# Second mixture of experts: six result buffers, rows six tiles at a time, sums in step with the tiles, and the last thirteen tiles behind a jump

## The chip, the cores and the metric

The kernel is one program on one core of a Trainium2 chip. The metric is the device time of one execution, in microseconds. Three executions of the kernel before took 852.63, 846.68 and 850.48 us; the median is 850.48 us. The profile is of a further execution.

## What is computed

The model has two layers; each adds an attention-like block and then a mixture of experts to x, of shape 16 x 128 x 256, float32. The change touches only the mixture of the second layer. There 2048 tokens (16 blocks of 128) choose 6 of 32 experts each. Cut to what matters:

```python
idx, w = _route(xf, Wr, br)                  # 2048 tokens, 6 of 32 experts, weights
gate = zeros((T, E)).at[arange(T)[:, None], idx].add(w)
def step(acc, ew):                           # over the 32 experts
    w1, w2, g = ew
    h = jnp.square(jax.nn.relu(xf @ w1.T)) @ w2.T
    return (acc + g[:, None] * h, None)
acc, _ = jax.lax.scan(step, zeros_like(xf), (W1, W2, gate.T))
x = x + jnp.tanh(g_ffn[1]) * (shared + acc)
```

xf is the normalised x. W1 is 128 x 256 for each expert and W2 256 x 128. Which experts a token takes depends on the data.

## The kernel before, in words

The kernel computes an expert only for the tokens that chose it. For each of the 16 blocks the router's result gives every (token, choice) a place in a table `sent` in device memory, sorted so that each tile of 128 rows belongs to one expert; GpSimd scatters the normalised rows there (line 961). A row carries the six expert numbers and the six places to which its results go. An expert's last tile may be partly filled, so up to NT1 = 16 x 6 + 31 = 127 tiles exist, and the program runs all 127, whatever the data; tiles without tokens write into a part of the result table that nobody reads. `state["used"]` holds the number of rows that were given out, tiles times 128.

The loop over tiles is written out in the program, `for t in range(NT1)`. Its steps and their lines in the profile:

- Every GRP = 4 tiles, SP loads the rows of four tiles (`got`, L1131, pool tag "big", 4 buffers) and ScalarE loads four weight offsets into registers (L1123). VectorE then finds the place of each row's result (`mine`, `to_f`, `to`, L1135 to L1145).
- Every two tiles (a pair): ScalarE copies each tile's expert weights out of the resident table (`wt`, L1155); TensorE turns the rows (L1158); VectorE copies them out of PSUM (`xts`, L1160); TensorE multiplies by W1 (`eh`, L1165); ScalarE takes the relu (`er`, L1173); VectorE multiplies relu by its input (`ehs`, L1175); TensorE multiplies by W2 (`eo`, L1177); ScalarE copies the result to SBUF (`ey`, L1185, three buffers).
- For each tile, GpSimd scatters 128 result rows of 1 KB to their places in the table `parts` (L1186). This is an indirect DMA, issued on GpSimd's queue.
- The sums. The blocks are in GROUPS of 4, 4, 4, 2, 1 and 1. All results of a group's blocks lie in the first last_tile(c) = 6 x (last block + 1) + 31 tiles. `combine(c)` stands six tiles behind that (or behind the last tile). For each block of the group SP loads three parts of 128 x 2 x 256 (`part`, L1109, four buffers), VectorE does six multiply-and-adds into x (L1115), and SP stores the block (L1118).

A framework puts these on the engines. Each engine works through its own queue in order. A scheduler sets that order when the program is built, close to the program's order with some interleaving; waits are semaphores that the framework adds, for data and for buffers to come free. [...]

Of the kernel before, what the change touches and what calls it, by code (L numbers as in the profile page):

```python
# [11 lines left out]
I32 = mybir.dt.int32  # L12
# [31 lines left out]
GRP = 4  # L44
# [7 lines left out]
def flamingo(ctx: ExitStack, tc: tile.TileContext, a: dict, out: bass.AP):  # L52
# [1039 lines left out]


    results, summed = [], []
    chunk = 0
# [5 lines left out]
    def combine(c):  # L1101

        n = P * TOPK1
        for b in range(*GROUPS[c]):
            for k0 in range(0, TOPK1, 2):
                part = work.tile([P, 2, D], F32, tag="act", name=f"part{b}_{k0}", bufs=4)
                at = NT1 * P + b * n
                src = parts[at : at + n, :].rearrange("(p k) d -> p k d", k=TOPK1)
                load = nc.sync.dma_start(out=part, in_=src[:, k0 : k0 + 2])  # L1109
                for ins in results[last_tile(c) :]:  # L1110
                    tc.declare_no_dep(load.ins, ins.ins, reason="later tiles have no row of a chunk that is summed")
                after(load, results[: last_tile(c)], "a chunk's results come from any of the first tiles")
                summed.append(load)
                for k in range(2):
                    V.scalar_tensor_tensor(  # L1115
                        xs[b], part[:, k, :], gates[:, b, k0 + k : k0 + k + 1], xs[b], ALU.mult, ALU.add
                    )
            nc.sync.dma_start(out=out[b], in_=xs[b])  # L1118

    for t in range(NT1):  # L1120
        if t % GRP == 0:
            n = min(GRP, NT1 - t)
            offsets = nc.values_load_multi_w_load_instructions(  # L1123
                table[0:1, t : t + n],
                engines=[mybir.EngineType.Activation],
                min_val=0,
                max_val=(E1 - 1) * W1_ROW,
                skip_runtime_bounds_check_because="the table holds numbers of experts times their weights' size",
            )[1]
            rows = work.tile([P, GRP, ROW], F32, tag="big", name=f"got{t}", bufs=BIGS)[:, :n]  # L1130
            load = nc.sync.dma_start(out=rows, in_=sent[t * P : (t + n) * P, :].rearrange("(g p) d -> p g d", p=P))  # L1131
            after(load, scatters, "a tile's rows come from any batch")

            mine = small.tile([P, GRP, TOPK1], F32, tag="mine", name=f"mine{t}", bufs=4)[:, :n]
            V.tensor_tensor(  # L1135
                mine,
                rows[:, :, D : D + TOPK1],
                owner[:, t : t + n].unsqueeze(2).to_broadcast([P, n, TOPK1]),
                ALU.is_equal,
            )  # L1140
            V.tensor_tensor(mine, mine, rows[:, :, D + TOPK1 :], ALU.mult)
            to_f = small.tile([P, GRP], F32, tag="to_f", name=f"to_f{t}", bufs=3)[:, :n]
            V.tensor_reduce(to_f, mine, AX.X, ALU.add)
            to = small.tile([P, GRP], U32, tag="to", name=f"to{t}", bufs=8)[:, :n]
            V.tensor_tensor(to, to_f, aside[:, t : t + n], ALU.max)  # L1145

        if t % 2 == 0:
            pair = range(t, min(t + 2, NT1))
            m = len(pair)
            tp = bank(("tr", "sc")[t // 2 % 2], f"xt{t}", 2)  # L1150
            eh = bank("mm", f"eh{t}", 2)
            eo = bank("so", f"eo{t}", 2)
            wt = work.tile([P, 2, W1_ROW], F32, tag="xT", name=f"wt{t}", bufs=4)
            for i, u in enumerate(pair):
                S.copy(wt[:, i], wts[:, bass.ds(offsets[u % GRP], W1_ROW)])  # L1155
                for kc in range(KC):
                    at = i * D + kc * P
                    T.transpose(tp[:, at : at + P], rows[:, u % GRP, kc * P : (kc + 1) * P], ident)  # L1158
            xt = work.tile([P, 2 * D], F32, tag="h", name=f"xts{t}", bufs=3)
            V.tensor_copy(xt[:, : m * D], tp[:, : m * D])  # L1160

            for i in range(m):
                for kc in range(KC):
                    cols = slice(kc * P, (kc + 1) * P)
                    T.matmul(  # L1165
                        eh[:, i * P : (i + 1) * P],
                        lhsT=wt[:, i, cols],
                        rhs=xt[:, i * D + kc * P : i * D + (kc + 1) * P],
                        start=(kc == 0),
                        stop=(kc == KC - 1),  # L1170
                    )
            r = work.tile([P, ROW], F32, tag="row", name=f"er{t}", bufs=8)[:, : m * P]
            S.activation(r, eh[:, : m * P], AF.Relu)  # L1173
            h = work.tile([P, D], F32, tag="xn", name=f"ehs{t}", bufs=3)[:, : m * P]
            V.tensor_tensor(h, r, eh[:, : m * P], ALU.mult)  # L1175
            for i in range(m):
                T.matmul(  # L1177
                    eo[:, i * D : (i + 1) * D],
# [74 lines left out]
```

## Time and profile before

| | |
|---|---|
| median of three runs | 850.48 us |
| profiled execution, time | 854.49 us |
| its span, first to last instruction | 852.7 us |
| mean granted TensorE clock | 0.918 |
| first row load of the second mixture issued | 644.65 us |
| first scatter starts | 657.22 us |
| 114th scatter starts | 820.48 us |
| 127th and last scatter starts | 841.60 us |
| last store issued | 850.03 us |
| scatters of results | 127, median 969 ns on GpSimd, 4.2 us from issue to landing |
| row loads | 31 of 536 KB and one of 402 KB |
| part loads | 48 of 256 KB, landing 2.7 / 2.8 us (min / median) |
| multiply-and-adds of the sums | 96 |

How to read it: times within the execution run from the start of the span. The time of an execution is a little longer than its span (854.49 against 852.7). A line of a group shows the source line, engine, operation, out<-in, shapes and count, then busy time and mean duration in ns of one, then the idle time before these instructions and who ended it.

### The profile page before, as it was taken

How to read it: one execution, taken by the hardware profiler on the slowest of the kernel's cores; microseconds unless marked ns; L12 is line 12 of the kernel's file. 1: busy time of each engine (PE TensorE's matmuls, PEld its weight loads, DVE VectorE, ACT ScalarE, POOL GpSimd, SP SyncE). 2: the span in 40 equal slices, each digit the busy share in tenths (PEclk: the TensorE clock that was granted, in tenths of full speed). 3: DMA queues.
4: the chain of work that ended last, by engine and by line, in shares of the span. 5: the costliest groups of instructions: out<-in, count | busy, mean ns of one | idle time of the engine just before them, and what ended most of it. 6: DMA issues, size and time to landing. Idle time of an engine off the chain costs nothing.

```text
span 852.7 us, 12578 instructions
## 1 busy us (share of the span) xinstructions
PE 747.0 (88%) x4032; PEld 524.1 (61%) x4032; DVE 548.6 (64%) x1660; ACT 375.4 (44%) x814; POOL 345.8 (41%) x339
## 2 busy tenths in 40 slices
PE   6999978989999999999899989698787989788862
PEld 3444444577675787565568657455456878677851
DVE  5999994337336755669647955756764546665675
ACT  2010046124424766552445344245435767666651
POOL 3766604200606000011640173046452767665663
PEclk8999979989999999999969969759978999998996
DMA  8999996122523233711331142523125657888586
GB/s 271 328 364 262 271 254 161 36 80 75 179 93 104 66 104 94 188 29 35 107 90 32 30 120 70 149 65 103 52 78 164 232 196 230 270 287 278 190 270 207
DMA packets 136513, 132.47 MB, mean 155 GB/s; under 512 B 43392, under 2 KB 119968, under 8 KB 136320
## 3 DMA queue, kind: packets, MB, share of 16 engines
q1 hardware_dynamic: 122576, 93.40, 39.3%
q0 software_dynamic: 13776, 38.23, 12.6%
q8 instruction: 32, 0.52, 0.3%
q14 instruction: 33, 0.27, 0.1%
q10 hardware_dynamic: 96, 0.05, 0.0%
HBM read 66.01 MB, written 65.62 MB: 154 GB/s over the span
## 4 chain that ended last, share of the span: by engine, by line
PE 49%; DVE 20%; DMA 11%; issue 7%; POOL 6%; ACT 5%; ACTq 0%; POOLq 0%; SPq 0%; DVEq 0%
PE y L328 7%; PE sc L844 5%; PE gu L771 4%; POOL parts L1186 4%; DMA part<-parts 4%; PE pg L606 3%; PE pu L606 3%; PE pt L865 3%; DMA parts<-ey,to 3%; PE os L658 3%; PE eo L781 3%; PE eo L1177 2%; DMA got<-sent 2%; PE avT L879 2%; ACT ex L858 2%
## 5 line engine op out<-in xcount | busy, mean ns | idle before, releaser
L1186 POOL DMA_INDIRECT parts<-ey,to x127 | 125.1, 985 | 74.4 <-ACT ey L1185 38.8
L961 POOL DMA_INDIRECT sent<-row,dst x96 | 93.3, 972 | 135.3 <-DVE dst L598 103.8
L858 ACT ACTIVATE ex<-sc,mn 128x128 f32<-128x128 f32 x256 | 71.8, 381 | 51.6 <-DVE mn L852 51.5
L801 POOL DMA_INDIRECT part<-parts,places x32 | 31.2, 975 | 143.7 <-DMA keys<-in_ctxT 86.2
L328 PE MATMUL y<-kv,toe 128*128 128x512 f32 x192 | 85.3, 599 | 0.0
L1177 PE MATMUL eo<-wt,ehs 128*128 128x256 f32 x254 | 68.9, 408 | 18.2 <-DVE ehs L1175 18.0
L320 POOL TENSOR_TENSOR kv<-cT 128x1024 f32<-128x1024 f32 x32 | 60.6, 1895 | 38.2 <-PE y L328 33.5
L1155 ACT COPY wt<-wts 128x512 f32 x127 | 72.2, 618 | 4.5 <-DVE x L622 1.5
L714 POOL DMA_INDIRECT sent<-row,places x32 | 31.2, 975 | 104.5 <-DVE places L493 41.0
L1165 PEld LDWEIGHTS eh<-xts,wt 128*128 128x128 f32 x508 | 69.4, 206 | 5.5 <-issue 2.5
L1165 PE MATMUL eh<-xts,wt 128*128 128x128 f32 x508 | 70.7, 291 | 1.2 <-DVE xts L1160 1.1
L606 PE MATMUL pg<-xT_s,wts 128*128 128x512 f32 (+1 forms) x160 | 66.4, 536 | 0.5 <-DVE silu L421 0.4
L606 PE MATMUL pu<-xT_s,wts 128*128 128x512 f32 (+1 forms) x160 | 64.0, 520 | 2.2 <-DVE row L200 2.2
L1177 PEld LDWEIGHTS eo<-wt,ehs 128*128 128x128 f32 x254 | 47.1, 200 | 28.3 <-DVE ehs L1175 18.4
L658 PE MATMUL os<-wts,hs 128*128 128x256 f32 x256 | 63.3, 382 | 0.0
L844 PE MATMUL sc<-keys,xT_at 32*128 32x256 f32 x256 | 61.6, 446 | 0.0
L328 PEld LDWEIGHTS y<-kv,toe 128*128 128x128 f32 x192 | 36.1, 193 | 41.5 <-issue 29.4
L1115 DVE SCALAR_TENSOR_TENSOR x<-part,gates,x 128x256 f32<-128x256 f32 x96 | 44.5, 479 | 23.4 <-DMA part<-parts 22.8
L1185 ACT COPY ey<-eo 128x512 f32<-128x512 f32 x64 | 37.2, 583 | 49.4 <-DMA parts<-ey,to 18.7
L1160 DVE COPY xts<-xt 128x512 f32<-128x512 f32 x64 | 43.1, 681 | 22.3 <-PE eh L1165 11.4
L658 PEld LDWEIGHTS os<-wts,hs 128*128 128x128 f32 x256 | 47.7, 191 | 15.2 <-issue 9.4
L852 DVE TENSOR_REDUCE mn<-sc 128x4 f32<-128x512 f32 x64 | 42.3, 682 | 16.8 <-PE sc L844 16.5
(246 smaller groups left out, 1393.6 us busy)
## 6 DMA issues: line engine op xcount, KB each, us to landing
sent<-keys SPq DMA_DIRECT2D x1, 17018.0 KB
got<-sent SPq DMA_DIRECT2D x31, 536.0 KB
part<-parts SPq DMA_DIRECT2D x48, 256.0 KB
sent<-keys SPq DMA_DIRECT2D x2, 2944.0 KB
got<-sent SPq DMA_DIRECT2D x22, 256.0 KB
parts<-ey SPq DMA_DIRECT2D x22, 256.0 KB
wts<-in_sw SPq DMA_DIRECT2D x3, 1024.0 KB
wts<-in_w SPq DMA_DIRECT2D x3, 1024.0 KB
```

The lines of the kernel that those rows point to most:

```text
L320: G.tensor_tensor(kv, c[:, :, hs].unsqueeze(3).to_broadcast(full), c[:, :, hs].unsqueeze(2).to_broadcast(full), ALU.mult)
L328: T.matmul(y[:, lb * TOK : (lb + 1) * TOK], lhsT=t[:, off : off + P], rhs=kv[:, kc * HALF : (kc + 1) * HALF].rearrange("p b i j -> p (b i ...
L606: T.matmul(ps, lhsT=w(kc), rhs=xT[:, kc, :n], start=(kc == 0), stop=(kc == KC - 1))
L658: T.matmul(o[:, k * D : (k + 1) * D], lhsT=hs[j][:, t * P : (t + 1) * P], rhs=wC[:, j, :], start=False, stop=(j == SH0 - 1 and k == len(ts ...
L844: T.matmul(scs[r][:, kc * D : (kc + 1) * D], lhsT=xT[rows, kc, cols], rhs=kz[rows, kc].rearrange("p m t -> p (m t)"), start=False, stop=(k ...
L858: S.activation(ex[:, i, :], scs[r][:, at : at + P], AF.Exp, bias=mn[:, i : i + 1], scale=-1.0)
L961: ins = G.indirect_dma_start(out=sent[:, :], out_offset=bass.IndirectOffsetOnAxis(ap=dst[:, t, k : k + 1], axis=0), in_=row, in_offset=None,)
L1115: V.scalar_tensor_tensor(xs[b], part[:, k, :], gates[:, b, k0 + k : k0 + k + 1], xs[b], ALU.mult, ALU.add)
L1155: S.copy(wt[:, i], wts[:, bass.ds(offsets[u % GRP], W1_ROW)])
L1165: T.matmul(eh[:, i * P : (i + 1) * P], lhsT=wt[:, i, cols], rhs=xt[:, i * D + kc * P : i * D + (kc + 1) * P], start=(kc == 0), stop=(kc == ...
L1177: T.matmul(eo[:, i * D : (i + 1) * D], lhsT=h[:, i * P : (i + 1) * P], rhs=wt[:, i, KC * P :], start=True, stop=True,)
L1186: ins = G.indirect_dma_start(out=parts[:, :], out_offset=bass.IndirectOffsetOnAxis(ap=to[:, t % GRP : t % GRP + 1], axis=0), in_=y[:, t % ...
```

## The change

1. GRP becomes 6: rows of six tiles in a load, six offsets at a time, owner steps on six tiles. The owner steps are put behind the pair's other work in the program, and the first of them must follow the copy `xts` of the group's first pair.
2. `ey` takes its buffers in turn from two tags of three buffers each: six pairs of tiles can hold results.
3. The sums of groups 0, 1 and 2 (blocks 0 to 11) are no longer fetched group-wise in `combine`. After a tile, one part is fetched (two for group 2) if the tile lies at least last_tile + 6 in; it waits for the results up to five tiles back, and is summed three tiles later (or when more than two wait).
4. The tile loop becomes a function `tiles1(t0, t1)`. Tiles 0 to 113 (SURE = 114) always run. Then all engines load `used` into a register, and tiles 114 to 126 run only if more than 114 x 128 rows were given out. On the other side of the jump the semaphores are raised by what the tiles left out would have raised; GpSimd first waits for the scatters before it raises theirs.
5. Blocks 12 to 15 are summed behind that jump by `sum_last`: three loads into one buffer ("big"), six scalings by the gates on ScalarE in place, one reduce over the six on VectorE, one add into x, one store.

The built program has in SP's queue, behind the jump: block 12's first load, the store of block 10, 12's other loads, 13's first, the store of block 11, 13's and 14's loads, the store of block 12, 15's loads, three stores. On VectorE seven of the old sums, of blocks 10 and 11, stand behind the jump as well.

The diff, cut to its core:

```diff
-GRP = 4
+GRP = 6
+SURE = 114
+FEW = 3
...
+    used_i = base.tile([P, 1], I32, tag="used_i", name="used_i")
+    V.tensor_copy(used_i, state["used"])
...
-    def combine(c):
-        n = P * TOPK1
-        for b in range(*GROUPS[c]):
-            for k0 in range(0, TOPK1, 2):
-                part = work.tile([P, 2, D], F32, tag="act", name=f"part{b}_{k0}", bufs=4)
...
-                for k in range(2):
-                    V.scalar_tensor_tensor(
-                        xs[b], part[:, k, :], gates[:, b, k0 + k : k0 + k + 1], xs[b], ALU.mult, ALU.add
-                    )
-            nc.sync.dma_start(out=out[b], in_=xs[b])
+    def load_results(part, b, k0, n_tiles):
...
+        load = nc.sync.dma_start(out=part, in_=src[:, k0 : k0 + 2])
...
+        after(load, results[:n_tiles], "a chunk's results come from any of the first tiles")
+        summed.append(load)
+    todo = [(b, k0) for b in range(GROUPS[FEW][0]) for k0 in range(0, TOPK1, 2)]
+    fetched = []
+    def fetch(t):
+        b, k0 = todo.pop(0)
+        part = work.tile([P, 2, D], F32, tag="act", name=f"part{b}_{k0}", bufs=4)
+        load_results(part, b, k0, min(t - 5, len(results)))
+        fetched.append((t, b, k0, part))
+    def add_fetched():
+        _, b, k0, part = fetched.pop(0)
+        for k in range(2):
+            V.scalar_tensor_tensor(xs[b], part[:, k, :], gates[:, b, k0 + k : k0 + k + 1], xs[b], ALU.mult, ALU.add)
+        if k0 + 2 == TOPK1:
+            nc.sync.dma_start(out=out[b], in_=xs[b])
+    def sum_last(b):
+        part = work.tile([P, TOPK1, D], F32, tag="big", name=f"part{b}", bufs=BIGS)
+        for k0 in range(0, TOPK1, 2):
+            load_results(part[:, k0 : k0 + 2], b, k0, len(results))
+        for k in range(TOPK1):
+            S.activation(part[:, k, :], part[:, k, :], AF.Copy, scale=gates[:, b, k : k + 1])
+        s = work.tile([P, D], F32, tag="xn", name=f"sum{b}", bufs=3)
+        V.tensor_reduce(s, part.rearrange("p k d -> p d k"), AX.X, ALU.add)
+        V.tensor_tensor(xs[b], xs[b], s, ALU.add)
+        nc.sync.dma_start(out=out[b], in_=xs[b])
-    for t in range(NT1):
+    def tiles1(t0, t1):
+        for t in range(t0, t1):
...
-            y = work.tile([P, 2, D], F32, tag="ey", name=f"ey{t}", bufs=3)
+                y = work.tile([P, 2, D], F32, tag=("ey", "got0")[t // 6 % 2], name=f"ey{t}", bufs=3)
...
+                follow(ins, turned_rows, "not needed before")
...
-        while chunk < len(GROUPS) and t + 1 >= min(NT1, last_tile(chunk) + 6):
-            combine(chunk)
-            chunk += 1
+            while fetched and (fetched[0][0] <= t - 3 or len(fetched) > 2):
+                add_fetched()
+            for _ in range(2 if todo and group(todo[0][0]) + 1 == FEW else 1):
+                if todo and t + 1 >= last_tile(group(todo[0][0])) + 6:
+                    fetch(t)
+    tiles1(0, SURE)
+    while fetched:
+        add_fetched()
+    used = nc.values_load(used_i[0:1, 0:1], min_val=0, max_val=NT1 * P, ...)
+    with tc.If(used > SURE * P):
+        tiles1(SURE, NT1)
+    for b in range(GROUPS[FEW][0], B):
+        sum_last(b)
```

## Prediction

> **What bounds the kernel now.** I read the page first (span 852.7 us), then the chain of waits. From 643 us on the chain stays in the second mixture, so I took that stage alone: the busy time in three stretches, GpSimd's timeline, the waits, the end of the chain, and the groups by shape.
>
> ```profile
> 657.20:736.30 79.10, 71.63 (x490) 64.73 (x488) 39.75 (x126) 57.38 (x119) 57.20 (x60) 0.98 0.67 210
> 736.30:841.60 105.30, 79.71 (x488) 70.39 (x488) 71.54 (x198) 62.53 (x126) 66.96 (x68) 0.92 0.82 267
> 841.60:852.70 11.10, 0.00 (x0) 0.00 (x0) 4.33 (x9) 0.00 (x0) 0.96 (x1) 0.50 0.39 134
> ```
>
> Columns: stretch, length, then busy us and instructions of PE, weight loads, DVE, ACT, POOL, the granted clock, DMA share, GB/s. The first stretch has tiles and no sums, the second both, the third only the last sums. No engine is full in the second, yet its tiles are slower.
>
> ```profile
> 657.22 0.96 POOL L1186 DMA_INDIRECT parts<-ey,to  x1 [14.17 <-ACT ey L1185]
> 658.49 0.97 POOL L1186 DMA_INDIRECT parts<-ey,to  x1 [0.31 <-issue]
> ...
> 740.57 1.19 POOL L1186 DMA_INDIRECT parts<-ey,to  x1 [3.34 <-ACT ey L1185]
> ...
> 841.60 0.97 POOL L1186 DMA_INDIRECT parts<-ey,to  x1 [0.30 <-issue]
> ```
>
> Each tile is one GpSimd scatter, 0.97 us and 0.30 us to the next: 1.275 us. From the first start (657.22) to the 127th (841.60) are 184.38 us; 126 x 1.275 is 160.65, so stalls are 23.7 us. To the 114th (820.48) the same sum gives 163.26 - 144.08 = 19.2 us of stalls, only about 3.8 of them before tile 60, where the sums begin.
>
> ```profile
> POOL parts L1186 <- ACT ey L1185: 38.8, 19, 14.2
> DVE mine L1135 <- DMA got<-sent: 30.7, 17, 4.8
> ...
> DVE x L1115 <- DMA part<-parts: 22.8, 14, 3.8
> ACT ey L1185 <- DMA parts<-ey,to: 18.7, 11, 4.0
> ```
>
> The stalls are waits for ey (the 14.2 is the start). ey comes late for two reasons: its three buffers are not yet scattered (18.7 us), and VectorE stands at a sum whose rows have not landed (22.8), with the next tiles' copies queued behind it; the 30.7 us at mine block ehs in the same way.
>
> ```profile
> 841.60 2.41 DMA parts<-ey,to
> ...
> 844.14 2.75 DMA part<-parts
> ...
> 846.91 0.49 DVE x L1115
> ...
> 849.51 0.48 DVE x L1115
> ```
>
> So the tail behind the last scatter's start is 11.1 us: landing, load, six sums, the store.
>
> ```profile
> L1115 DVE SCALAR_TENSOR_TENSOR x<-part,gates,x 128x256 f32<-128x256 f32 x96 | 44.5, 479 | 23.4 <-DMA part<-parts 22.8
> ...
> L406 DVE TENSOR_REDUCE mask_e<-eq_e 128x128 f32<-128x768 f32 x3 | 4.4, 1456 | 0.0
> ...
> L596 DVE TENSOR_REDUCE dstf<-eq_e 128x24 f32<-128x768 f32 x3 | 2.8, 945 | 0.0
> ```
>
> These three price the old and the new sum.
>
> **Part by part, on the profiled execution.**
>
> *Is the jump taken?* Counting the reference's routing on its inputs, tokens per expert rounded up to 128 give 113 tiles. SURE is 114, so the last 13 are left out: 13 x 1.275 = **-16.6 us** on the GpSimd queue, which paces the stage.
>
> *Rows six at a time.* The first load grows from 536 to 804 KB. Its row is 4.18 us; if all of that scaled it would cost 2.1 more, if none, 0. I take 1.3, plus one more transpose in front of the first eo (1.94 us / 8 = 0.24): **+1.5**. Later loads are issued up to four groups ahead (24 tiles instead of 16) and stay hidden; without that cover VectorE's 30.7 us at got would come back. The owner test is put behind the first xts, so it no longer stands in front of ehs while rows are under way.
>
> *Six result buffers.* The wait for scatters (18.7) goes: a scatter lands in 4.2 us (median), six pairs give 15 us. What is late next is PE. From the chain, 16 eh take 1.78 us, 8 eo 1.90, 12 xt 1.31, so a pair costs 0.89 + 0.95 + 0.44 = 2.28, 1.14 us a tile at full clock and 1.24 at 0.92. Both are under 1.275, so GpSimd keeps the pace, with little left for catching up. Before tile 60 I leave 2 us of the 3.8.
>
> *Sums in step.* Blocks 0 to 7 are fetched one part a tile at tiles 60-71 and 84-95, summed three tiles later. VectorE's tile without sums is 0.685/2 + 0.414/2 + 0.70/6 = 0.67 us (xts, ehs, the four owner steps per six); two sums add 0.96: 1.63, or 0.35 over the pace, 4.2 us for a burst of 12. The other end is 0: unlinked sums in the trace follow each other at 0.41 us, which leaves 1.49, and run-ahead from the buffers covers the rest. I take 2.5 a burst, 5 in all. Blocks 8 to 11 come two parts a tile at 108-113. In VectorE's order ehs110 stands behind the first sum of block 8, whose load waits for the scatter of tile 102: landing 4.2, issue 0.4, load 2.8, sum 0.5, ehs 0.4, eo and ey about 2 give 10.3 us against 10.2 for eight tiles; ehs112 behind seven more sums is a bit later: 1. Stalls to the last scatter are then 2 + 5 + 1 = 8 (bounds 2 and the old 19.2): 8 - 23.7 = **-15.7**.
>
> *The last scatter* therefore starts at 841.6 - 16.6 - 15.7 + 1.5 = 810.8.
>
> *The tail* now holds four blocks instead of about one, since SP and VectorE may fetch blocks 12-15 only behind the jump, and these wait for all results. Landing 2.4. Then register load and branch on every engine, and GpSimd raising the counts of the 13 scatters left out: the trace has no jump; a register load is 0.31 to 0.71 us, so 0.4 at least; at most 12.6, the refill from the first got (644.65) to the first scatter. It is nearest to a register load, as nothing refills: 1. The rest of block 10 and 11 (7 sums, 3.5 us on VectorE) runs beside the landing and the next load. Block 12's three loads: SP issues them with one store between, 1.1, last landing 2.75, two scalings at 0.42 (ACT h<-relu 128x256): 4.7. Then VectorE: reduce and add per block. The reduce takes 1536 elements, six apart: twice mask_e's 1456 ns (also six per result) is 2.9 us; twice dstf's is 1.9. I take 2.9, the same reading order. With an add of 0.41 that is 3.3 a block, more than the six old sums (6 x 0.479 = 2.9): ScalarE's 24 scalings save VectorE nothing. Four blocks: 13.2; the store 2.7. Part 15's loads are queued behind out12, but land before VectorE is through with 14. Sum 2.4 + 1 + 4.7 + 13.2 + 2.7 = 24.0, so **+12.9** (with the cheap reduce, loads then in the way, 20.5).
>
> Total: -16.6 - 15.7 + 1.5 + 12.9 = **-17.9 us**: span 834.8, that execution 836.6 instead of 854.49. It was 4 us over the median of 850.48, so I forecast 850.48 - 17.9, about **833**.
>
> [...]
>
> [...] POOL's scatters are 0.963 us at least and 1.257 at most, with sums beside them. [...]
>
> **Rivals.**
> - *A, the above:* own range 826 to 840. Chance 0.50.
> - *B, everything hides:* stalls 2 and tail 20.5: -6 - 3.5, so 823. For it: stretches of 20 scatters at 1.275 flat between sums. Against: mask_e's reduce. Chance 0.16.
> - *C, the gain is eaten by transfers.* In a burst a tile moves 137 KB of rows, 131 of results, 262 of parts, about 44 of output: 574 KB in 1.275 us, 450 GB/s, where the trace's fullest 20 us moved 334 at share 0.98. If stalls stay at the old 19.2, +11.2 gives 844; so does a jump of 12.6. Against: rows are loaded long before need; over tiles 60-108 the demand is 20.2 MB, 60.5 us at 334 GB/s, in 61.2. Chance 0.28.
> - *D, slower: the jump isn't taken.* It decides from 115 used tiles. Then the pipe drains, refills (12.6) and sends 13 tiles more (16.6): +29, so 862. Against: the count of 113; two experts would have to spill into another tile. The counts are data, and the trace doesn't show them. Chance 0.06.
>
> **How the numbers follow.** 833 is A's. B's floor with no cost at the jump is 821; C with a dear reduce and stalls together ends at 847. 821 to 847 leaves out D and the far end of C. One per cent (842 to 859 counts as the same) is about what a measurement of this kernel can tell. Faster: A, B and 0.08 of C, 0.74; same: 0.16 of C; slower: D and 0.04 of C, 0.10.
>
> **What would show it.** 114 scatters; first start near 658.7, last near 811; between them 1.275 us mostly, gaps of a few us near tiles 60-75 and 85-100; ACT's wait for scatters nearly gone; four reduces near 2.9 us in the last 15 us; from the last scatter to the end 24 us. Wrong if: 127 scatters; 19 us of gaps; or a reduce under 2 us with a tail under 20.

## The result, and the profile after

The changed kernel took 842.41 us (median of 19 runs, 839.58 to 847.6), the kernel before, beside it on the same chip, 848.25 us (19 runs, 842.3 to 852.63). The ratio is 0.9944, 95% interval 0.9924 to 0.9963: 4.7 us by the ratio, 5.8 by the medians. The forecast was 833, or -17.9 us. The change did what it says, with 114 scatters, and brought a quarter to a third of what was forecast. Some executions of a kernel are slower as a whole; ratios leave them out, and the one profile that fell on such an execution (jump_alone_2) isn't read.

The profiled execution took 845.23 us, its span is 843.5 (before: 854.49 and 852.7), TensorE's mean clock 0.908. The three stretches again (length; busy us and instructions of PE, weight loads, DVE, ACT, POOL; granted clock, DMA share, GB/s):

```profile
656.26:732.65 76.39, 70.13 (x487) 63.48 (x485) 38.41 (x104) 58.16 (x123) 58.10 (x60) 1.00 0.66 207
732.65:814.93 82.28, 63.42 (x383) 55.61 (x383) 52.70 (x140) 45.88 (x95) 52.91 (x53) 0.89 0.76 248
814.93:843.50 28.57, 0.00 (x0) 0.00 (x0) 17.54 (x19) 10.08 (x24) 1.11 (x1) 0.50 0.56 181
```

Here the first stretch ends with the start of the 61st scatter (before: of the 60th). It goes at GpSimd's pace: 76.39 us is 60 x 1.275 - 0.1, no gap at all. The last 54 have gaps (82.28 against 53 x 1.275 = 67.6), and the third stretch, in which TensorE has nothing left to do, has grown from 11.10 to 28.57 us. GpSimd's timeline, with the scatters before which it waited longest (the figure in brackets is the idle time; its usual 0.30 belongs to the pace):

```profile
656.26 0.97 POOL L1219 DMA_INDIRECT parts<-ey,to  x1 [14.79 <-ACT ey L1203]
...
738.09 1.22 POOL L1219 DMA_INDIRECT parts<-ey,to  x1 [3.19 <-ACT ey L1203]
...
754.15 1.20 POOL L1219 DMA_INDIRECT parts<-ey,to  x1 [3.07 <-ACT ey L1203]
...
761.81 0.96 POOL L1219 DMA_INDIRECT parts<-ey,to  x1 [2.64 <-ACT ey L1203]
...
778.09 0.98 POOL L1219 DMA_INDIRECT parts<-ey,to  x1 [3.42 <-ACT ey L1203]
...
814.93 1.11 POOL L1219 DMA_INDIRECT parts<-ey,to  x1 [0.30 <-DMA parts<-ey,to]
```

From the first start to the 114th are 158.67 us, 113 x 1.275 is 144.1: gaps of 14.6 us, at tiles 62, 72, 76 and 86 above all (tiles are counted from 0). In the waits, ScalarE's 18.7 us for scattered buffers are gone. What ey waits for now is TensorE's eo, and VectorE still waits for parts:

```profile
DVE x L1133 <- DMA part<-parts: 18.1, 11, 3.6
...
POOL parts L1219 <- ACT ey L1203: 31.1, 14, 14.8
...
ACT ey L1203 <- PE eo L1194: 39.8, 33, 5.4
```

The end of the chain of waits (start, us, what):

```profile
820.86 0.33 SPq L1112
...
822.74 5.04 DMA part<-parts
...
828.08 2.80 DVE sum L1145
...
837.54 2.74 DVE sum L1145
```

5.9 us pass from the last scatter's start (814.93) to the first load of block 12; another 7.2 to the first reduce; four reduces and adds take 12.6, the store 2.8: 28.6 us.

Between the two profiles the span fell by 9.2 us: 13 scatters -16.6, gaps -9.1 (23.7 to 14.6), tail +17.4, and -1.0 for a first scatter that starts earlier.

### The profile page after: what moved, and what is told of

Its sections match the earlier page's. It is cut to its first block, busy times and chain, and to the rows that moved or that the text cites. A ratio compares the mean times of both kernels' runs of the same rounds, so it can differ in the third digit from the quotient of the medians.

```text
span 843.5 us, 12155 instructions
## 1 busy us (share of the span) xinstructions
PE 726.8 (86%) x3928; PEld 506.5 (60%) x3928; DVE 539.7 (64%) x1579; ACT 367.8 (44%) x811; POOL 332.7 (39%) x326
## 4 chain that ended last, share of the span: by engine, by line
PE 53%; DVE 19%; DMA 8%; issue 7%; ACT 7%; POOL 3%; ACTq 1%; SPq 0%; DVEq 0%; POOLq 0%
PE y L330 7%; PE sc L846 5%; PE gu L773 4%; PE eo L1194 4%; PE pg L608 4%; PE pu L608 3%; PE eh L1182 3%; PE pt L867 3%; PE os L660 3%; PE eo L783 3%; DMA part<-parts 2%; DMA parts<-ey,to 2%; PE avT L881 2%; PE p L608 2%; ACT ex L860 2%
## 5 line engine op out<-in xcount | busy, mean ns | idle before, releaser
L1219 POOL DMA_INDIRECT parts<-ey,to x114 | 112.1, 984 | 62.4 <-ACT ey L1203 31.1
L1194 PE MATMUL eo<-wt,ehs 128*128 128x256 f32 x228 | 63.7, 412 | 21.3 <-DVE ehs L1192 21.1
L1172 ACT COPY wt<-wts 128x512 f32 x114 | 66.3, 620 | 13.0 <-issue 8.3
L608 PE MATMUL pg<-xT_s,wts 128*128 128x512 f32 (+1 forms) x160 | 68.1, 548 | 0.4 <-DVE silu L423 0.4
L1182 PEld LDWEIGHTS eh<-xts,wt 128*128 128x128 f32 x456 | 62.2, 201 | 7.2 <-ACT wt L1172 3.6
L1182 PE MATMUL eh<-xts,wt 128*128 128x128 f32 x456 | 64.7, 286 | 1.6 <-ACT wt L1172 1.5
L330 PEld LDWEIGHTS y<-kv,toe 128*128 128x128 f32 x192 | 35.9, 191 | 41.2 <-issue 29.1
L1194 PEld LDWEIGHTS eo<-wt,ehs 128*128 128x128 f32 x228 | 41.8, 201 | 29.3 <-DVE ehs L1192 24.5
L1177 DVE COPY xts<-xt 128x512 f32<-128x512 f32 x57 | 38.6, 685 | 29.2 <-PE xt L1175 21.6
L854 DVE TENSOR_REDUCE mn<-sc 128x4 f32<-128x512 f32 x64 | 42.3, 682 | 15.8 <-PE sc L846 15.5
L1203 ACT COPY ey<-eo 128x512 f32<-128x512 f32 x57 | 33.4, 585 | 40.0 <-PE eo L1194 39.8
L773 PEld LDWEIGHTS gu<-xts,wt 128*128 128x128 f32 x368 | 46.3, 196 | 7.1 <-issue 2.5
```

The lines of the kernel that those rows point to most:

```text
L330: T.matmul(y[:, lb * TOK : (lb + 1) * TOK], lhsT=t[:, off : off + P], rhs=kv[:, kc * HALF : (kc + 1) * HALF].rearrange("p b i j -> p (b i ...
L608: T.matmul(ps, lhsT=w(kc), rhs=xT[:, kc, :n], start=(kc == 0), stop=(kc == KC - 1))
L773: T.matmul(gu[:, half * D + u * P : half * D + (u + 1) * P], lhsT=wt[:, u, w : w + P], rhs=xt[:, u * D + kc * P : u * D + (kc + 1) * P], s ...
L1182: T.matmul(eh[:, i * P : (i + 1) * P], lhsT=wt[:, i, cols], rhs=xt[:, i * D + kc * P : i * D + (kc + 1) * P], start=(kc == 0), stop=(kc == ...
L1194: T.matmul(eo[:, i * D : (i + 1) * D], lhsT=h[:, i * P : (i + 1) * P], rhs=wt[:, i, KC * P :], start=True, stop=True,)
L1219: ins = G.indirect_dma_start(out=parts[:, :], out_offset=bass.IndirectOffsetOnAxis(ap=to[:, t % GRP : t % GRP + 1], axis=0), in_=y[:, t % ...
```

## The experiments

Every kernel ran beside the kernel before. The upper part of the table is from chips on which that took 846 to 848 us, the lower part from others, on which it took 967 to 971 us; the lower part's ratios are set beside each other only. The table is read from each profile: start of the first scatter, gaps (start to start less 1.275 us, added up to the 114th), tail (last scatter's start to the end of the span).

| kernel | ratio to before, 95% | first | gaps | tail | span |
|---|---|---|---|---|---|
| before | | 657.2 | 19.2 | 11.1 | 852.7 |
| after | 0.9944 (0.9924 to 0.9963) | 656.3 | 14.6 | 28.6 | 843.5 |
| before_again | one run, 843.14 us | 653.5 | 15.3 | 11.5 | 841.4 |
| three_ey | 0.9970 (0.9937 to 1.0002) | 655.8 | 17.2 | 29.1 | 846.2 |
| fetch_later | 0.9883 (0.9831 to 0.9936) | 654.0 | 10.5 | 27.8 | 836.3 |
| no_jump | 1.0088 (1.0053 to 1.0122) | 655.4 | 12.4 | 23.1 | 853.7 |
| rows4 | 1.0002 (0.9981 to 1.0023) | 654.3 | 15.1 | 29.2 | 842.7 |
| tail_muladd | 0.9920 (0.9891 to 0.9948) | 657.4 | 11.8 | 25.7 | 839.0 |
| tail_free | 0.9866 (0.9831 to 0.9900) | 654.1 | 12.7 | 25.6 | 836.5 |
| both | 0.9858 (0.9817 to 0.9898) | 655.4 | 9.6 | 25.6 | 834.7 |
| *other chips:* after_again | 0.9817 (0.9773 to 0.9861) | 741.2 | 38.8 | 28.1 | 952.1 |
| main_alone | 0.9953 (0.9923 to 0.9983) | 736.3 | 40.1 | 12.5 | 954.1 |
| main_alone_2 | 0.9964 (0.9927 to 1.0000) | 741.0 | 42.0 | 12.2 | 959.9 |
| jump_alone | 0.9936 (0.9907 to 0.9965) | 740.6 | 51.9 | 29.5 | 966.0 |
| last_ahead | 0.9814 (0.9772 to 0.9856) | 738.8 | 40.1 | 24.8 | 947.7 |
| best | 0.9783 (0.9744 to 0.9821) | 741.1 | 39.6 | 24.1 | 948.9 |
| best_2 | 0.9766 (0.9715 to 0.9817) | 738.0 | 38.5 | 25.4 | 946.0 |
| loads_only | 0.9807 (0.9730 to 0.9883) | 737.7 | 36.9 | 26.5 | 945.2 |
| sums_only | 0.9764 (0.9703 to 0.9825) | 740.2 | 36.4 | 25.9 | 946.5 |

after, tail_muladd and tail_free are the same program up to the 114th scatter. Their gaps are 14.6, 11.8 and 12.7: that is how far profiles of one thing differ, and a difference of under 3 us between two single rows means nothing.

**before_again: the kernel before once more.**

> The kernel before once more, for a second profile. Theory (its first profiled execution, 854.5 us, was one of its longer ones: some 6 us over the median of its 19 runs): a span of 843 to 850 us, with fewer than 20 us of gaps between scatters in place of 23.7. Rival (a profile costs some us by itself): a span of 851 to 854 again, gaps of 22 to 25 us.

Span 841.4 us; gaps to the 127th scatter 15.8 us (126 x 1.275 = 160.65 taken from 653.49 to 829.94), where the first profile had 23.7.

```profile
653.49:729.78 76.29, 69.43 (x490) 63.35 (x488) 39.98 (x125) 57.12 (x119) 57.23 (x60) 1.00 0.68 219
729.78:829.94 100.16, 79.03 (x488) 69.19 (x488) 70.41 (x196) 61.62 (x126) 66.56 (x67) 0.93 0.82 277
829.94:841.40 11.46, 0.00 (x0) 0.00 (x0) 5.30 (x11) 0.00 (x0) 0.97 (x1) 0.54 0.44 153
```

From the 60th scatter's start to the last one's are 100.16 us in place of 105.30, and before it 76.29 in place of 79.10. 59 x 1.275 are 75.2, so the gaps up to there, 3.8 us in the first profile, of which the forecast left 2, are 1.1 us in this one. The first profile was of a long execution: 854.49 us, where the 19 runs have their median at 848.25.

**three_ey: results in three buffers again.**

```diff
-y = work.tile([P, 2, D], F32, tag=("ey", "got0")[t // 6 % 2], name=f"ey{t}", bufs=3)
+y = work.tile([P, 2, D], F32, tag="ey", name=f"ey{t}", bufs=3)
```

> The changed kernel with its results in three buffers again instead of six; rows six at a time, sums in step, jump and tail as changed. Theory (VectorE's in-order queue makes the stalls: a sum in step waits for a part, and the pairs behind it are late whatever the number of result buffers): the stall-free stretch before tile 60 gets its 3 to 4 us of gaps between scatters back, the stretch from tile 60 changes by at most 2 us, so +3 to +6 us against the changed kernel's 842.4. Rival (the run-ahead of six buffers is what holds the bursts down to 3 to 6 us a decade): gaps of over 25 us from scatter 0 to 113 in place of 14.6, +10 us or more. Rival (buffers are worth nothing, since the scatters' own queue is the bound): within 1.5 us.

By ratios it is 2.2 us slower than the whole change (0.9970 against 0.9944; the intervals overlap). In its trace ScalarE waits 11.4 us for scattered buffers again, the tiles before the 60th have 4.3 us of gaps in place of none, and the gaps after it are 12.9, within what the three profiles of the changed kernel show. This is the theory's mechanism, with 2 us in place of 3 to 6: in these profiles the buffers clear the stretch without sums and do nothing for the bursts.

**fetch_later: results twelve tiles back for groups 0 and 1.**

```diff
+    def lag(b):
+        return 6 if group(b) + 1 == FEW else 12
-        load_results(part, b, k0, min(t - 5, len(results)))
+        load_results(part, b, k0, min(t + 1 - lag(b), len(results)))
-                if todo and t + 1 >= last_tile(group(todo[0][0])) + 6:
+                if todo and t + 1 >= last_tile(group(todo[0][0])) + lag(todo[0][0]):
```

> The changed kernel with the parts of groups 0 and 1 fetched against results twelve tiles back instead of six, from six tiles later on; number of parts, loads, sums and bytes unchanged, group 2 unchanged. Theory (the sum waits for a load that itself waits for a recent scatter and then lands in 4 to 6 us): VectorE's waits for parts fall from 18.1 us to under 9, gaps between scatters from 14.6 to 5 to 9 us, time -5 to -9 us against the changed kernel. Rival (the DMA engines are full in the bursts, 0.76 of their time busy, and the rows' 804 KB stand in SyncE's queue ahead of the parts): the same bytes in as long a stretch, within 2 us. Rival (VectorE's own work is the bound in the bursts): within 2 us, and VectorE's waits for parts fall without the gaps falling.

0.9883 against 0.9944, 5 us, though the intervals overlap a little; gaps 10.5 (9.6 in the kernel `both`) where the changed kernel's three profiles have 13.0 in the mean and 11.8 at least. So the direction is probably the theory's, the size (5 to 9 us of gaps, waits under 9 us) is not: VectorE still waits 15.0 us for parts. The traces say why. First VectorE and TensorE of the changed kernel at the start of the first burst, then the clock in two windows:

```profile
730.49 0.48 DVE L1133 SCALAR_TENSOR_TENSOR x<-part,gates,x 128x256 f32<-128x256 f32 x1 [3.44 <-DMA part<-parts]
...
734.24 0.48 DVE L1133 SCALAR_TENSOR_TENSOR x<-part,gates,x 128x256 f32<-128x256 f32 x1 [2.17 <-DMA part<-parts]
734.65 0.41 DVE L1192 TENSOR_TENSOR ehs<-er,eh 128x256 f32<-128x256 f32 x1
```

```profile
735.11 3.78 PE L1194 MATMUL eo<-wt,ehs 128*128 128x256 f32 x8 [5.51 <-DVE ehs L1192]
```

```profile
732.50:739.30 6.80, 4.19 (x11) 3.48 (x12) 4.15 (x12) 1.48 (x3) 3.15 (x3) 0.50 0.96 330
739.30:748.80 9.50, 9.34 (x69) 8.34 (x67) 6.79 (x18) 7.62 (x17) 7.09 (x8) 1.00 0.95 315
```

VectorE reaches the first sum at 727.1 and stands there until 730.49, since the load was issued only at 727.57, when the scatter of tile 54 (725.01) had landed. Behind the second wait stands an ehs, so TensorE idles 5.51 us, its clock drops to 0.5 for 6.8 us, and in that time it gets 11 matmuls done (eight of them, for eo, take 3.78 us, 0.47 each; 0.24 in the next window). GpSimd works off the ready results meanwhile and then waits 3.19 us, at tile 62. The gaps at tiles 72 and 86 begin like it: VectorE stands 3.55 us at a sum until 751.10, and 2.36 and 1.62 us until 772.39 and 775.10; TensorE idles 3.20 us from 748.8 and 3.91 us from 772.1, GpSimd runs dry, and the clock stands at 0.5 from 753.0 and from 776.9. The changed kernel's chain of waits goes the same way, at tile 62 and again at tile 86:

```profile
726.28 2.42 DMA parts<-ey,to
...
728.77 5.38 DMA part<-parts
...
734.24 0.48 DVE x L1133
734.73 0.34 DVE ehs L1192
...
735.11 3.78 PE eo L1194 x8
...
770.91 4.10 DMA part<-parts
...
775.10 0.48 DVE x L1133
775.58 0.34 DVE ehs L1192
...
775.97 2.93 PE eo L1194 x8
```

A scatter lands, the part lands 5.4 us after its load's issue (2.75 in the tail of the kernel before), the sum, ehs, eo: each waits for the one ahead. In fetch_later:

```profile
728.16 0.48 DVE L1136 SCALAR_TENSOR_TENSOR x<-part,gates,x 128x256 f32<-128x256 f32 x1 [2.91 <-DMA part<-parts]
...
731.29 0.48 DVE L1136 SCALAR_TENSOR_TENSOR x<-part,gates,x 128x256 f32<-128x256 f32 x1 [2.02 <-DMA part<-parts]
```

```profile
732.17 2.07 PE L1197 MATMUL eo<-wt,ehs 128*128 128x256 f32 x4 [4.86 <-DVE ehs L1195]
```

The sum stands six tiles further down the program (tile 69), and VectorE is there at 725.3, when the scatter of tile 54 has just landed: it runs ahead of GpSimd by as much as the buffers allow and uses up the distance. The load is not issued earlier for it. The later place shortened these waits by 0.5 and 0.15 us only.

In this profile TensorE's clock is 0.50 for 6.8, 3.4 and 3.4 us (from 732.5, 753.0 and 776.9), each time within or up to 0.9 us behind one of these idle times, 5.51, 3.20 and 3.91 us. In the kernel before, idle times of 2.3 us (from 788.0) and 2.1 us (from 825.9) were followed by 3.4 us at 0.50 too, and one of 3.0 us (from 735.1) was not: the clock is 1.00 there (the ends of matmuls are modelled in a profile, so these three are rough). How much of a gap is the wait and how much the slow clock after it isn't separated; no run changed the clock alone.

**rows4: rows four tiles at a time.**

```diff
-GRP = 6
+GRP = 4
-            if t % GRP == 0:
-                n = min(GRP, NT1 - t)
+            if t == t0 or t % GRP == 0:
+                g0, n = t, min(GRP - t % GRP, t1 - t)
```

> The changed kernel with its rows loaded four tiles at a time (536 KB) instead of six (804 KB); six result buffers, sums in step, jump and tail as changed. Theory (VectorE's order and the parts' wait for scatters make the stalls): the first load is shorter, -1 to -1.5 us at the first scatter; gaps between scatters 12 to 17 us; in all within 2 us of the changed kernel. Rival (the rows' large loads in SyncE's queue hold the parts up, landing 5 to 6 us in the bursts): gaps fall by 4 us or more and parts land in 3 us, -5 us or more. Rival (more loads and more of the groups' small VectorE work cost): +2 to +4 us.

1.0002 against 0.9944, so 5 us slower than the change: the third reading, at more than its price. The profile, 844.5 us, is of its shortest execution (median 847.4) and shows gaps of 15.1 and a tail of 29.2, so it doesn't hold those 5 us. What it shows is that smaller row loads don't shorten VectorE's waits for parts: 28.6 us in place of 17.8 (18.1 with the tail), the longest 9.7. By this one profile the rows in SyncE's queue are not what the parts wait for; SyncE's loads of parts waited 55.8 us for scatters here and 43.7 in the changed kernel.

**no_jump: all 127 tiles always.**

```diff
-    used = nc.values_load(...)
-    with tc.If(used > SURE * P):
-        tiles1(SURE, NT1)
+    tiles1(SURE, NT1)
```

> The changed kernel with all 127 tiles always run: no register load, no branch, the sums of the last four blocks behind tile 127 (they are still summed with ScalarE's scalings and a reduction). Theory: 13 scatters of 1.275 us come back, +16.6 us; the passage from last scatter to first load of the last blocks falls from 5.9 us by 2 to 3.5 (no semaphores raised, no register load), so +12 to +15 us against the changed kernel. Rival (the tiles behind the jump are cheap, since their scatters carry rows that nobody reads and run beside the first of the last loads): +8 us or less. Rival (the jump itself is free): +16 to +18 us.

1.0088 against 0.9944: +12.2 us, as the theory has it. From the 114th start to the 127th are 18.7 us, 2.2 more than 13 x 1.275, and the tail is 5.5 us shorter. The end of its chain shows where:

```profile
830.56 2.40 DMA parts<-ey,to
833.12 0.33 SPq L1112
```

Without a jump 2.56 us lie between the last scatter's start and the first load; with it 5.9 (after), 5.4, 6.7 and 6.1 (fetch_later, tail_free, both). At the jump line of the changed kernel, two GpSimd instructions stand out:

```profile
L1247 POOLq EVENT_SEMAPHORE  x4: 17/43/2270, 814.6 to 816.9; - x4
...
L1247 POOLq COMPARE_BRANCH  x1: 45/45/45, 814.4 to 814.4; - x1
...
L1247 POOLq INC_SWDGE_SEM  x1: 1422/1422/1422, 819.2 to 819.2; - x1
```

GpSimd branches in 45 ns, then waits until the last scatter has landed (816.86 to 819.13, 4.2 us behind its start, with part loads under way beside it), then spends 1.42 us raising the scatters' semaphores. SyncE had been at the loads since 817.6 and starts them at 820.86.

**tail_muladd, tail_free: other sums, another order.** The first puts six multiply-adds on VectorE in place of scalings and reduce, the second also issues the twelve loads in a row and stores from ScalarE's queue.

```diff
-            S.activation(part[:, k, :], part[:, k, :], AF.Copy, scale=gates[:, b, k : k + 1])
-        s = work.tile([P, D], F32, tag="xn", name=f"sum{b}", bufs=3)
-        V.tensor_reduce(s, part.rearrange("p k d -> p d k"), AX.X, ALU.add)
-        V.tensor_tensor(xs[b], xs[b], s, ALU.add)
+            V.scalar_tensor_tensor(xs[b], part[:, k, :], gates[:, b, k : k + 1], xs[b], ALU.mult, ALU.add)
```

> The changed kernel with the sums of the last four blocks made by six multiply-adds each on VectorE (0.41 us apiece in the sums in step) in place of six scalings on ScalarE, a reduction (2.77) and an add (0.4). Theory (in the tail a block's reduction can't begin before its sixth result has landed and is scaled): 24 multiply-adds of about 0.43 come to 10.3 us where reductions and adds took 12.6, and the first starts when the first part lands, at 3 us instead of 7.2 us after the first load, unless loads queued behind a store are then what ends last: -2 to -5 us. Rival (the loads of the tail, three a block with the store of an earlier block queued between them, set the end as soon as VectorE is faster): -1 us to +1 us.

> The same sums by multiply-adds on VectorE, and the twelve loads of the last four blocks issued one after the other, with those blocks' stores in ScalarE's queue, so that no load stands behind a store that waits for VectorE (the stores of two earlier blocks, already done with, stay). Theory: first part at 3 us after the first load, 24 multiply-adds, store 2.8: tail 28.6 to about 21 to 23 us, -5 to -8 us against the changed kernel, and -3 us or more against the kernel with multiply-adds alone. Rival (twelve loads of 262 KB at once fill the DMA engines: 3.1 MB at 250 GB/s are 12.6 us): the last part lands 13 us after the first load, tail about 24 to 25 us, -3 to -5 us.

The tails are 25.7 and 25.6 us, 2.9 below the change's: a block costs VectorE six times 0.49 in place of 3.2, and the start is earlier. In the traces the order of loads and stores brings nothing on top of that, and the 21 to 23 us expected for tail_free were wrong: the store of block 11 was not done with, it waits for that block's last sum (820.88), and eight of the twelve loads are issued behind it, from 821.78 on. From 822.94 on the multiply-adds of tail_free follow each other:

```profile
822.94 10.80 DVE L1145 SCALAR_TENSOR_TENSOR x<-part,gates,x 128x256 f32<-128x256 f32 x22 [1.18 <-DMA part<-parts]
```

22 in 10.8 us, 0.49 each: VectorE carries it from there to the store, so the rival's full DMA engines are not what ends it. By ratios the two are 2.0 and 6.6 us faster than the change; the traces give 3 for either. The medians, 841.1 and 837.6 on one chip, would leave the order 3 us, but the two intervals overlap.

**both: later fetch and free tail.**

> The later fetch (results twelve tiles back for groups 0 and 1) together with the free tail (multiply-adds, loads ahead of stores). Theory: the two act in stretches that do not overlap, so the differences add up: -10 to -15 us against the changed kernel, 828 to 833 us, below the kernel before by over 1%. Rival (the later fetch moves the sums into the last tiles, where they meet the tail): the sum falls short by 3 us or more.

0.9858, 835.9 us: 7 us faster than the changed kernel by ratios, its interval below the changed kernel's. The profiles' terms do add (gaps 9.6, tail 25.6); the 10 to 15 us expected would have needed 5 to 8 us of each, where the profiles have 3 and 3. By ratios fetch_later and tail_free alone are 5.2 and 6.6 us faster, so both together fall 4.5 short of the sum, the rival's number; its mechanism isn't seen, the tail is 25.6 us with and without the later fetch. With intervals of 3 to 4.5 us either way this stays open.

**main_alone, jump_alone: the change in two halves**, each run twice, the second time beside the whole. The first has no jump and sums blocks 12 to 15 as before; the second puts `tiles1`, the jump and `sum_last` into the kernel before.

> One half of the change alone: six result buffers, rows six tiles at a time and sums of the first twelve blocks fetched in step, but all 127 tiles always run, without jump, and the last four blocks summed as in the kernel before. Theory (by the profiles so far, 13 scatters left out are worth 16.6 us and the tail behind the jump takes 28.6 us where the kernel before takes 11.1 to 11.5): the two cancel, so this is as fast as the whole change, 840 to 844 us, -4 to -7 against the kernel before, its gaps between scatters 12 to 15 us up to the 114th. Rival (the jump carries the whole gain and the rest gains nothing): within 2 us of the kernel before.

> The other half alone: the kernel before with rows four at a time, three result buffers and its sums of the first twelve blocks where they were, the last thirteen tiles behind the jump, and the last four blocks summed behind it with ScalarE's scalings and a reduction. Theory: -16.6 us of scatters and +17 us of tail, within 2 us of the kernel before, 846 to 850 us. Rival (the jump carries the gain): -4 to -8 us against the kernel before. Rival (without the rest the tail is longer): slower than before by 3 us or more.

> The changed kernel once more, on the chip on which its two halves run as well. Theory: 0.994 of the kernel before, gaps between scatters 11 to 15 us up to the 114th, tail 28 to 29 us. On a chip whose kernel before takes about 965 us the ratio would be as good or better, since its gaps are longer.

> The half without the jump again (six buffers, rows by six, sums in step, all tiles), beside the whole change on one chip. Theory: the two halves' gains do not add, since each half was measured at 0.993 to 0.996 of the kernel before and so was the whole: on a chip where the kernel before takes about 847 us, 0.993 to 0.996, and within 0.003 of the whole change. Rival: the whole is the product of the halves, 0.989, and this half lies 0.005 above it.

> The half with the jump alone again, beside the whole change on one chip. Theory (13 scatters, 16.6 us, against a tail longer by 17 us): within 0.003 of the kernel before on a chip where that takes about 847 us; lower where gaps between scatters are longer, since the thirteen tiles then cost more than 1.275 us each. Rival: the jump gains everywhere, 0.994 again.

Here the kernel before took 967.7 and 969.5 us and the question changed: with gaps of 39 to 52 us, not of 10 to 19. Half one 0.9953 and 0.9964, half two 0.9936 and 0.9851 (0.9798 to 0.9905; 0.9931 by the medians 962.8 and 969.5), the whole 0.9817. On these chips the jump does gain, 6 to 7 us by medians, as the rival had it; jump_alone_2's theory had allowed for it where gaps are long. The whole is better than either half beside it (medians 953.0 against 963.4 and 962.8). With 0.9936 for the jump the product of the halves is 0.990; why the whole is better than that isn't shown. The profiles agree in part: from the 114th start to the 127th main_alone_2 takes 20.6 us in place of 16.6 (947.69 - 927.12), and the tail of after_again is 15.9 longer. On the chips of the table's upper part the halves were not run. There the sum of profile terms is all there is: 16.6 to 18.7 us of tiles against a tail longer by 17.

**last_ahead, best: sums ahead of the jump.** The last sums are made into tiles of their own ahead of the jump, and again behind the 13 tiles where those run. best adds the later fetch, and sums two of the four blocks on TensorE.

```diff
+    sum_last(range(GROUPS[FEW][0], B))
     with tc.If(used > SURE * P):
         tiles1(SURE, NT1)
-    for b in range(GROUPS[FEW][0], B):
-        sum_last(b)
+        sum_last(range(GROUPS[FEW][0], B), "b")
```

> The kernel with the free tail (loads of the last four blocks one after the other, multiply-adds on VectorE, stores from ScalarE's queue), its last sums moved ahead of the jump into tiles of their own; they are made once more behind the thirteen tiles where those run. So no load waits until GpSimd has raised the skipped tiles' semaphores. Theory (from last scatter's start to the first load of block 12 the four kernels with a jump took 5.4, 5.9, 6.1 and 6.7 us, the one without 2.55): the passage falls to 2.5 to 3 us, -3 to -4 us against the free tail's 837.6. Rival (SyncE's queue is not free earlier, since the last parts of group 2 are issued and waited for until 5 us after the last scatter; or VectorE still adds them): -1 us or less.

> The later fetch, the last sums ahead of the jump, and of the last four blocks two summed on TensorE: ScalarE makes six diagonal matrices of a block's gates while the loads land, six matmuls add the scaled results up in PSUM, VectorE adds x once. Theory (VectorE's 24 multiply-adds, 10.8 us on end, carry the tail of the free version): 12 multiply-adds and two sums from PSUM come to 6.3 us, so -4 us, and -3 us for the passage: tail from the last scatter's start about 18 to 20 us, 827 to 832 us. Rival (the loads carry the tail: 3.1 MB at the 250 GB/s of the bursts are 12.6 us, then a store of 2.8): tail 21 to 23 us, 831 to 835 us.

> The later fetch, the last sums ahead of the jump and two of the last four blocks on TensorE again, beside the whole change on one chip. Theory: 827 to 832 us where the kernel before takes about 847, 0.977 to 0.982, tail from the last scatter's start 18 to 20 us. Rival (loads carry the tail): tail 21 to 23 us, 0.982 to 0.987.

The passage is 4.9 us (last_ahead) and 4.0 (best_2), not 2.5 to 3: the 1.42 us are off the path, but the last scatter lands 4.8 and 3.8 us behind its start, with parts in flight. The tails are 24.1 to 25.4, not 18 to 20. best_2's chain:

```profile
920.62 3.84 DMA parts<-ey,to
...
931.14 6.00 DMA part<-parts
...
937.27 4.50 PE sum L1156 x12
```

The loads carry it now, the rival's case, though its 21 to 23 us are too short as well: a store of block 11 that waits for VectorE stands between them (928.32), the last is issued at 931.1 and lands in 6.0 us. TensorE needs 4.5 us for the twelve matmuls that follow. Of the kernels that compute everything it is still the fastest on these chips, 0.9783 and 0.9766 where the whole change has 0.9817, but its intervals overlap that one's.

**loads_only, sums_only: which part of a sum costs.**

> The changed kernel with the 72 multiply-adds of the first twelve blocks left out (their outputs are x without the results); the parts are still fetched in step and land, and nobody reads them. Theory (VectorE's in-order queue: a sum waits for a part, the next pairs wait behind it): gaps between scatters fall from 12 to 15 us to under 5. Rival (the parts' transfers and the rows' large loads fill the DMA engines and hold rows and scatters up): gaps stay at 9 us or more.

> The changed kernel with the 36 fetches of the first twelve blocks left out: the multiply-adds stand where they were in VectorE's order, on a tile of zeros that is always there, so they wait for nothing and move nothing (outputs of these blocks are x without the results). Theory (the wait, not the work): gaps fall from 12 to 15 us to under 5, although VectorE's 35 us of multiply-adds stay. Rival (VectorE's own time is the bound in the bursts): gaps stay at 9 us or more.

Busy times from first to 114th scatter on these chips, of after_again, loads_only and sums_only:

```profile
741.15:924.05 182.90, 141.58 (x870) 124.40 (x868) 91.25 (x243) 105.52 (x218) 111.25 (x114) 0.92 0.62 201
```

```profile
737.73:918.70 180.97, 138.55 (x870) 122.69 (x868) 67.29 (x182) 105.86 (x218) 109.73 (x113) 0.93 0.60 199
```

```profile
740.17:920.68 180.51, 139.64 (x871) 123.58 (x869) 88.50 (x241) 105.04 (x218) 110.85 (x113) 0.92 0.48 158
```

VectorE loses 24 us of work in the one, the DMA engines a fifth of their traffic in the other, and the gaps fall from 38.8 to 36.9 and 36.4. Here the theory falls, with the rivals' reasons (their 9 us or more are met): neither waits for parts, nor their traffic, nor VectorE's work makes these gaps. Behind tile 60 they are 19.3 us in after_again and 16.6 and 16.2 without multiply-adds or fetches; ahead of it, where there are no sums, about 20 in all three. They lie in every stretch of ten tiles, and TensorE's mean clock from first to 114th scatter is 0.92 to 0.93 (0.94 to 0.97 in six of the upper part's profiles). Up to tile 60 after_again, last_ahead and loads_only, on three chips, have their large gaps at the same tiles (6, 14, 20, 26, 34, 38, 50, 56), so they follow the program's course, not chance. What makes them stays open, and since they cover everything, so does the split of the first chips' 13 us in the bursts between the waiting sum and the crowded DMA engines (share 0.95 to 0.96 in the windows above, parts landing in up to 6.1 us). One thing these runs do settle: without multiply-adds no scatter takes GpSimd over 0.98 us, with them up to 1.26 (sums_only, where nothing is fetched), so the multiply-adds alone lengthen a scatter by up to 0.3 us.

## Why the prediction was wrong

- *The jump is taken, -16.6.* Right: 114 scatters. Rival D is out.
- *Rows six at a time, +1.5.* From the load's issue to the first scatter 12.9 us (before: 12.6), so +0.3. Over seven kernels with the larger load it is 11.5 to 14.4, over two profiles of before 11.2 and 12.6: a difference that can't be told from none.
- *Six buffers.* Right in mechanism: ScalarE's wait for scatters is gone, and with it all gaps before tile 60, where 2 us had been left. But the step took the mean clock, 0.92, for a steady one, 1.24 us a tile. In the two windows above the clock is 0.50 and then 1.00, and a matmul for eo takes 0.47 us and then 0.24: if all of a pair's 2.28 us doubled like that, it would be 2.28 us a tile (an estimate from these), far over 1.275.
- *Sums in step, 5 us in the two bursts and 1 in group 2.* This step failed first. It compared rates, VectorE's 1.63 us a tile with the pace of 1.275, and took run-ahead as the cure. The traces show a wait: the first sums of a burst stand in VectorE's queue ahead of ehs, and their loads wait for a scatter that VectorE is 8 tiles ahead of (14 in fetch_later); TensorE idles 3.2 to 5.5 us, and its clock is then 0.50 for 3.4 to 6.8 us. Behind tile 60 the gaps are 12 to 15 us, where 6 had been left. How much of them is the wait for the scatter, how much the parts' slow landing and how much the clock isn't shown. Only group 2, which was worked out as a wait, cost no more than its price: 0.8 us, and 0.2 and 0.4 in the two other profiles, against 1.
- *The -15.7 for stalls* failed at its other end too. It was taken from one profile with 23.7 us; the next one has 15.8. With the mean of both, 19.8, and the 13.0 of three profiles after, it is -6.7. That the profiled execution was 4 us over the median was seen, and the whole difference was still taken over to the median.
- *The tail, +12.9.* This failed too, by 4.5 us. Landing, jump and semaphores: 5.9 against 3.4, from GpSimd's late landing (4.2 against 2.4) and 1.42 us of raising; the 1 us had been taken nearest to a register load. Loads and scalings of block 12: 7.2 against 4.7, since its last load landed in 5.04 us behind other loads, not in 2.75. Reduces and adds: 12.6 against 13.2, the store 2.8 against 2.7, both right. 28.6 in all, +17.4 on the first profile (11.1 before), +17.3 on the mean of the two.
- *The sum* with these sizes: -16.6 - 6.7 + 17.3 + 0.3 = -5.7 us, measured were 4.7 to 5.8. Four blocks' sums moved behind the last scatter cost what thirteen tiles save.
- *The rivals.* C's 844 is the nearest, for a reason that was half right: the gaps stayed large, but it priced a DMA bound over the whole stage, and the stage moved 248 GB/s at share 0.76; the crowding is in the bursts (share 0.96 and 0.95 in the two windows above). B's cheap tail did not come.
- *The jump itself.* In the changed kernel the branches took 45 to 373 ns, SyncE's 45 at 817.2, and its next instruction started at 817.4. What costs is the late landing (4.2 us) and the raising of the semaphores (1.42), for which the forecast had 2.4 and 1. Scatters took 1.35 us at most (before: 1.26).

## What to carry to other kernels

A sum placed in VectorE's in-order queue cost here the time from when VectorE was there to when the part was: 3.44 us at the first sum, and with the next one 5.51 us of TensorE behind them. Six result buffers took the gaps ahead of tile 60 away (none in place of three_ey's 4.3 us) and let VectorE run ahead into these waits: fetched against results twelve tiles back they were still 2.91 and 4.86 us. Work such a thing out as a wait, not as a rate. What was moved behind the last scatter was paid in full (a tail longer by 17.3 us), with what it takes to get past the jump (5.9 us to the first load, 2.56 without one): compare that bill with what the jump leaves out (16.6). And take the gain from two or more profiles, since the thing to be won may be one execution's bad luck: the gaps of the kernel before were 23.7 us in one and 15.8 in the next.

## What the runs showed of the hardware

- From the first scatter to the 114th of the changed kernel and to the 127th of the kernel before, TensorE's clock has seven stretches at 0.50 that end before the tail, 3.4 or 6.8 us long. Each began within an idle time of TensorE of 2.1 to 5.5 us or up to 1.2 us behind it; an idle time of 3.0 us in the kernel before was followed by none. In the changed kernel's first one a matmul for eo took 0.47 us where the next window had 0.24.
- GpSimd's INC_SWDGE_SEM behind the jump, which raises the semaphores for the scatters left out, took 1.42 us in after and in last_ahead, one on each kind of chip.
- The last scatter landed 2.4 us behind its start in no_jump, with no part load in flight, and 4.2 in after, 4.8 in last_ahead and 3.8 in best_2, with part loads in flight.
- With VectorE's multiply-adds beside them scatters took GpSimd 0.96 to 1.26 us in sums_only, where nothing is fetched; without them (loads_only) none took over 0.98.
- The kernel before took 847 us on some chips and 968 on others. In the changed kernel GpSimd's and VectorE's instructions took the same time each on both (985 against 982 ns a scatter, 686 against 685 ns a copy of xts, from first to 114th scatter); the difference is in waits and in TensorE's clock, 0.864 against 0.908 in the mean. Of the 109 us between these two profiles 85 lie ahead of the first scatter. Why is open.
